# Laying a state-space scan out by channels and states, in a kernel that runs it beside attention

## The chip, the cores and the metric

The kernel runs on one core of one Trainium2 chip. The core has five engines with a queue each, worked off in order: TensorE (PE) for matmuls, VectorE (DVE), ScalarE (ACT) and GpSimd (POOL) for elementwise work, SyncE (SP), which here issues nearly every DMA. The metric is the time of one execution in device microseconds. Of the kernel before, three runs took 6126.20, 6140.09 and 6140.57 us; the median is 6140.09.

## The reference

Two layers over x of 4 images, 128 channels, 64 x 64 pixels. Layer 0 normalises, convolves 3 x 3 by channel, and then treats the 128 channels as four chunks of 32 channels; each chunk of each image is one sequence of 4096 tokens for the same state-space block, with 64 inner channels d and 16 states n. Layer 1 is softmax attention (4 heads over 4096 tokens) and a mixture of 8 experts, 2 per token. What the change touches is this:

```python
delta = jax.nn.softplus(dt @ dt_proj_w.T + dt_proj_b)
A = -jnp.exp(A_log)
dA = jnp.exp(delta[..., None] * A)
dBu = delta[..., None] * Bm[:, :, None, :] * xin[..., None]
def step(h, inp):
    dA_t, dBu_t, C_t = inp
    h = dA_t * h + dBu_t
    y = jnp.einsum('bdn,bn->bd', h, C_t)
    return (h, y)
...
y = jnp.transpose(ys, (1, 0, 2)) + D_skip * xin
out = y * jax.nn.silu(z) @ out_proj_w.T
```

So delta and xin depend on the channel, B and C on the state, A on both; y is a sum over the states.

## The kernel before, in words

**Blocks and halves.** An image is cut into 8 blocks of 512 tokens. Two of the four chunks are worked on at a time: they are a half p of a block, and their 2 x 64 = 128 (chunk, channel) pairs lie on the 128 partitions. 4 images x 8 blocks x 2 halves x 16 give 1,024 scan units.

**A unit** is one state n of all 128 pairs. `fetched` (L724) loads B and C of that state for both chunks, repeated over the 64 channels, from `bcd` in DRAM into `rows` (512 KB). `decayed` (L734) makes da = exp(delta * A) on ACT. `scan` (L739) is three DVE operations of 128 x 512: h = B * du, where du = delta * xin; the scan along the tokens, starting from `states`; hc = C * h. `scanned` (L752) adds the skip term once the sum over the states, y, is complete.

**The sum over states** is made in PSUM: PE multiplies hc by the identity and accumulates 16 products per half. In image 0 each hc goes to PE. In the images after, POOL first adds each pair of hc, and PE gets 8 sums per half.

**The slot loop** (L1113) writes the order of the work out by hand: every engine's instructions are chained in the order in which they are recorded. There is one unit per slot. Beside the units run two lanes of tasks written as generators. A `yield` ends a half-slot: `advance(lane, True)` and `advance(lane, False)` each run one stage. Lane Y makes the inputs of later blocks: `first_norm` (y0), `conv` (xn), and `inputs` (L675) twice per block, where ACT makes softplus in the four steps e, e, ln, delta, and POOL finishes delta and du in five operations. Lane X finishes blocks after their scans: `closed` (L761) makes queries, keys and values, and `divided` and `finished` (L946) close the attention and do the experts. A stage that yields "short" (the experts' products and their evictions acc) lets lane X take a second pair of stages in a slot. Attention of an image starts when its last block is closed: per slot, four score products (sc), two exponentials of 128 x 1024 (pT) on ACT, and four products with the values (av, 64 columns each, two column tiles) a slot later. An fp32 product of PE is two records in the profile.

A slot before records, in this order: the sends collected so far and `rows` of the unit three slots ahead (SP); lane X's second half (its evictions); sc and pT; lane Y; the y products that are due, and `scanned`; the copy of the last state of the previous unit (ACT); da of the next unit (ACT); the three scan operations (DVE) and the pair's add (POOL); lane Y; av; lane X's first half (its products).

`until` (L1074) runs before a unit's rows are fetched: while the inputs of its half are not done, it runs the half-slots of both lanes, out of the slot's order.

## Time and profile before

| what | value |
|---|---|
| median of three runs | 6140.09 us |
| profiled execution: its own time, its span | 6135.26 us, 6133.5 us |
| granted TensorE clock, mean | 0.921 |
| busy: PE, DVE, ACT, POOL | 5188.5, 4197.3, 3952.4, 1925.1 us |
| DVE scan operations (h and the two forms of scan, hc) | 795.9, 1299.8 + 176.9, 801.2 us |
| POOL's adds of hc pairs | 384, 557.1 us |
| DMA moved | 928.55 MB, of it 1,024 x 512 KB rows |

The page has the busy time of each engine, a row of 40 slices of the span with the busy share in tenths, the chain of work that ended last followed back to its start, and the costliest groups of instructions with what ended the idle time before them. All lane and loop operations are recorded by one helper, so they share the line L445; they are told apart by the names of what they write and read. A window gives busy time by engine for a stretch of the span.

### The profile page before, as it was taken

The numbers are of one execution on the slowest core, as the hardware profiler recorded it, in microseconds if no ns is written. First come the engines' busy times: TensorE is split into PE (matmuls) and PEld (weight loads), VectorE is DVE, ScalarE is ACT, GpSimd is POOL, SyncE is SP. The second block draws the span as 40 slices with busy tenths as digits, with TensorE's granted clock in tenths as the row PEclk, the third lists the DMA queues.
The fourth block names the chain that finished last, engine by engine and source line by source line (L and its number), as shares of the span: only waits on it lengthen the run. The fifth ranks groups of instructions, "written<-read, shape, count | busy, mean of one in ns | idle before, by whom it ended". The sixth has DMA issues, their size and how long they took to land.

```text
span 6133.5 us, 60705 instructions
## 1 busy us (share of the span) xinstructions
PE 5188.5 (85%) x18378; PEld 2135.6 (35%) x18378; DVE 4197.3 (68%) x7155; ACT 3952.4 (64%) x6052; POOL 1925.1 (31%) x1757
## 2 busy tenths in 40 slices
PE   4666665698899989889999898999888898999996
PEld 2222222233333333333333333333333333333332
DVE  4888887788888877778888777888777772021112
ACT  3445544577777767677777676777777765655652
POOL 2334323444344334333444344344333320000000
PEclk7777777799999999999999999999999999999996
DMA  3444554555455535555555554555554542212210
GB/s 99 163 174 164 187 178 152 171 190 170 168 184 178 188 134 181 167 170 179 187 178 181 178 168 168 177 167 174 174 167 165 170 158 79 79 64 72 74 66 13
DMA packets 359137, 928.55 MB, mean 151 GB/s; under 512 B 37633, under 2 KB 120978, under 8 KB 358802
## 3 DMA queue, kind: packets, MB, share of 16 engines
q1 hardware_dynamic: 357634, 923.80, 44.7%
q8 instruction: 148, 2.42, 0.2%
q14 instruction: 187, 1.53, 0.1%
q10 hardware_dynamic: 1168, 0.80, 0.0%
HBM read 806.95 MB, written 100.66 MB: 148 GB/s over the span
## 4 chain that ended last, share of the span: by engine, by line
PE 43%; DVE 33%; ACT 12%; POOL 5%; issue 5%; DMA 2%; SPq 0%; DVEq 0%; ACTq 0%; POOLq 0%
PE av L445 18%; DVE h L445 15%; PE ps_X L445 10%; PE sc L445 9%; DVE hc L445 5%; DVE acc L445 5%; PE y L445 4%; ACT pT L445 3%; PE ps_Y L445 3%; DVE cm L445 3%; ACT L445 2%; ACT xt L445 2%; POOL rsX L445 2%; POOL rsY L445 1%; ACT da L445 1%
## 5 line engine op out<-in xcount | busy, mean ns | idle before, releaser
L445 ACT ACTIVATE pT<-sc 128x1024 f32<-128x1024 f32 x2048 | 1986.7, 1024 | 881.2 <-PE sc L445 876.3
L445 PE MATMUL av<-pT,v 128*64 128x512 f32 x8192 | 2027.1, 616 | 0.0
L445 DVE TENSOR_TENSOR_SCAN h<-da,state,h 128x512 f32<-128x512 f32 x896 | 1299.8, 1451 | 244.0 <-ACT da L445 157.8
L445 PE MATMUL sc<-qs,ks 128*128 128x512 f32 x4096 | 1335.2, 444 | 124.5 <-ACT pT L445 77.4
L445 POOL TENSOR_TENSOR hc<-hc 128x512 f32<-128x512 f32 x384 | 557.1, 1451 | 1707.3 <-DVE hc L445 1542.9
L445 PEld LDWEIGHTS sc<-qs,ks 128*128 128x128 f32 x4096 | 714.3, 192 | 726.5 <-ACT pT L445 367.8
L445 PE MATMUL y<-hc,ident 128*128 128x512 f32 x1280 | 804.2, 718 | 181.7 <-DVE hc L445 172.5
L445 PEld LDWEIGHTS av<-pT,v 128*64 128x64 f32 x8192 | 506.9, 139 | 1168.0 <-issue 1140.3
L445 DVE TENSOR_TENSOR hc<-rows,h 128x512 f32<-128x512 f32 x1024 | 801.2, 782 | 70.9 <-DVE h L445 1.4
L445 DVE TENSOR_TENSOR h<-rows,du 128x512 f32<-128x512 f32 x1024 | 795.9, 777 | 32.3 <-POOL du L445 29.2
L445 ACT ACTIVATE da<-delta,amat 128x512 f32<-128x512 f32 x1024 | 750.2, 734 | 25.8 <-DVE h L445 24.3
L445 DVE SCALAR_TENSOR_TENSOR acc<-ps_X,pr,acc 128x128 f32<-128x128 f32 x1024 | 358.4, 350 | 304.6 <-PE ps_X L445 276.8
L445 ACT ACT_TABLE_LOAD x318 | 408.0, 1283 | 101.8 <-PE sc L445 92.1
L445 POOL TENSOR_SCALAR rsX<-mvX 128x4 f32<-128x4 f32 x97 | 52.4, 540 | 1224.3 <-DVE mvX L445 1222.7
L445 PE MATMUL ps_X<-w_ew,xf 128*128 128x512 f32 x512 | 304.3, 678 | 126.0 <-DVE acc L445 123.9
L445 PEld LDWEIGHTS y<-hc,ident 128*128 128x128 f32 x1280 | 260.3, 222 | 419.8 <-DVE hc L445 302.8
L445 DVE RECIPROCAL rden<-ps_X 128x8 f32<-128x8 f32 x64 | 13.1, 205 | 566.9 <-PE ps_X L445 566.9
L445 ACT COPY state<-h 128x1 f32<-128x1 f32 x896 | 176.3, 197 | 269.6 <-DVE h L445 269.2
L445 ACT ACTIVATE xt<-ps_Y,shiftY,rsY 128x128 f32<-128x128 f32 x380 | 142.9, 460 | 174.3 <-POOL shiftY L445 158.2
L445 DVE TENSOR_TENSOR_SCAN h<-da,h 128x512 f32<-128x512 f32 x128 | 176.9, 1382 | 57.0 <-ACT da L445 45.8
L445 POOL TENSOR_SCALAR rsY<-mvY 128x4 f32<-128x4 f32 x95 | 43.5, 458 | 532.7 <-DVE mvY L445 528.0
L445 PE MATMUL ps_Y<-ident,xt 128*128 128x128 f32 x380 | 74.7, 329 | 159.8 <-ACT xt L445 159.5
(197 smaller groups left out, 4766.6 us busy)
## 6 DMA issues: line engine op xcount, KB each, us to landing
rows<-bcd SPq DMA_DIRECT2D x1024, 512.0 KB, 4.2
ks<-kd SPq DMA_DIRECT2D x256, 512.0 KB, 5.6
v<-vd SPq DMA_DIRECT2D x256, 256.0 KB, 5.9
qs<-qd SPq DMA_DIRECT2D x64, 512.0 KB, 5.8
pairs<-xn SPq DMA_DIRECT2D x128, 128.5 KB, 2.4
qd<-hi SPq DMA_DIRECT2D x32, 512.0 KB, 6.8
qd<-lo SPq DMA_DIRECT2D x32, 512.0 KB, 5.9
vd<-vst SPq DMA_DIRECT2D x32, 512.0 KB, 7.4
```

Source lines behind the costliest of these rows:

```text
L445: return lambda *args, **kw: queued(op(*args, **kw))
```

## The change

Rows are laid out anew. A unit is now 8 channels with all 16 states of one chunk; eight units cover a chunk's 64 channels, sixteen a half. B and C depend on the state and the chunk alone, so one tile `bcs` (512 KB) holds both for eight units, while `rows` now brings delta and du of the unit's 8 channels, repeated over the 16 states. For that, `inputs` writes delta and du into one tile `dd` and sends it to DRAM as `ddd`, each row twice (1 MB), two slots after POOL's operations (four yields more). da is computed from the fetched delta, so it reads `rows` too. The sum over states crosses partitions: PE multiplies hc by the 0/1 matrix `sel`, 32 columns wide; the four units of a group write to four strips of 32 partitions of y, and four groups accumulate. POOL's pair adds are gone in all images. The channels are reordered on the partitions to match (`place`).

In the slot, the state copy and da of the next unit now come before sc and pT, and the scan comes before lane X's evictions, unless the stage is a short one. e and ln move to the scratch buffers of lane Y, `lost` shares du's place; da has two buffers and hc six.

```diff
@@ -92,7 +92,7 @@
-    amat = const.tile([P, NST], F32, name="amat")
+    amat = const.tile([P, P // NST], F32, name="amat")
...
@@ -697,60 +697,81 @@
         bcd = dram.tile([2, NST, 2 * BLK], F32, name="bcd", bufs=4)
         send(bcd.rearrange("c n (k q) -> (c n k) q", k=2), bc)
-        e = mix.tile([P, BLK], F32, name="e")
+        dd = mix.tile([P, 2, BLK], F32, name="dd")
+        delta, du = dd[:, 0, :], dd[:, 1, :]
+        e = tmp("Y", "e")
         scalar.activation(e, ps, AF.Abs, bias=dtb)
         scalar.activation(e, e, AF.Exp, scale=-1.0)
-        ln = mix.tile([P, BLK], F32, name="ln")
+        ln = tmp("Y", "ln")
         scalar.activation(ln, e, AF.Ln, bias=1.0)
-        delta = mix.tile([P, BLK], F32, name="delta", bufs=2)
         scalar.activation(delta, ps, AF.Relu, bias=dtb)
         yield
         yield
-        lost = mix.tile([P, BLK], F32, name="lost")
+        lost = du
         gpsimd.tensor_scalar(lost, e, 1.0, -1.0, ALU.add, ALU.add)
         gpsimd.tensor_sub(lost, e, lost)
         gpsimd.tensor_add(ln, ln, lost)
         gpsimd.tensor_add(delta, delta, ln)
-        du = mix.tile([P, BLK], F32, name="du", bufs=2)
         gpsimd.tensor_mul(du, delta, xin)
-        in_of[b, i, p] = xin, zs, delta, du, bcd
+        yield
+        yield
+        yield
+        yield
+        ddd = dram.tile([P, 2, 2 * BLK], F32, name="ddd", bufs=4)
+        send(ddd, dd.rearrange("p k q -> p (k q)")[:, None, :].to_broadcast([P, 2, 2 * BLK]))
+        in_of[b, i, p] = xin, zs, ddd, bcd
         yield
         yield
         yield
     states = [mix.tile([P, 2, NST], F32, name=f"state{k}") for k in range(2)]
-    def fetched(b, i, p, n):
-        bcd = in_of[b, i, p][4]
+    def fetched(b, i, p, k):
+        ddd, bcd = in_of[b, i, p][2:]
+        if k % 8 == 0:
+            w = mix.tile([P, 2, BLK], F32, name="bcs", bufs=2)
+            sync.dma_start(
+                out=w.rearrange("p k q -> p (k q)"),
+                in_=bcd[k // 8][None].to_broadcast([P // NST, NST, 2 * BLK]),
+            )
+            chunk[0] = w
         w = mix.tile([P, 2, BLK], F32, name="rows", bufs=4)
+        at = 32 * (k % 4) + 8 * (k // 4)
         sync.dma_start(
             out=w.rearrange("p k q -> p (k q)"),
-            in_=bcd[:, n, :][None].to_broadcast([DI, 2, 2 * BLK]),
+            in_=ddd[at : at + 8].rearrange("d c q -> (d c) q")[:, None, :].to_broadcast(
+                [NST, P // NST, 2 * BLK]
+            ),
         )
-        return w
-    def decayed(b, i, p, n):
-        da = mix.tile([P, BLK], F32, name="da", bufs=3)
-        scalar.activation(da, in_of[b, i, p][2], AF.Exp, scale=amat[:, n : n + 1])
+        return w, chunk[0]
+    chunk = [None]
+    def decayed(k, w):
+        da = mix.tile([P, BLK], F32, name="da", bufs=2)
+        scalar.activation(da, w[:, 0, :], AF.Exp, scale=amat[:, k % 8 : k % 8 + 1])
         return da
-    def scan(b, i, p, n, w, da):
-        du = in_of[b, i, p][3]
+    def scan(b, i, p, k, w, bc, da):
         h = mix.tile([P, BLK], F32, name="h", bufs=3)
-        vector.tensor_mul(h, w[:, 0, :], du)
+        vector.tensor_mul(h, bc[:, 0, :], w[:, 1, :])
         vector.tensor_tensor_scan(
-            out=h, data0=da, data1=h, initial=0.0 if i == 0 else states[b % 2][:, p, n : n + 1],
+            out=h, data0=da, data1=h, initial=0.0 if i == 0 else states[b % 2][:, p, k : k + 1],
             op0=ALU.mult, op1=ALU.add,
         )
-        hc = mix.tile([P, BLK], F32, name="hc", bufs=5)
-        vector.tensor_mul(hc, w[:, 1, :], h)
+        hc = mix.tile([P, BLK], F32, name="hc", bufs=6)
+        vector.tensor_mul(hc, bc[:, 1, :], h)
         return h, hc
     def scanned(b, i, p, y):
-        xin, zs, delta, du, bcd = in_of.pop((b, i, p))
+        xin, zs = in_of.pop((b, i, p))[:2]
         vector.scalar_tensor_tensor(xin, xin, dsk, y, ALU.mult, ALU.add)
         gpsimd.tensor_mul(zs, xin, zs)
         gated[b, i, p] = zs
@@ -1109,14 +1130,20 @@
     units = [(b, i, p, n) for b, i in blocks for p in range(2) for n in range(NST)]
     rows, decays, old, due = {}, {}, None, deque()
-    even, y_of, waiting, groups, image, slot = None, {}, None, None, 0, 0
+    terms, y_of, waiting, groups, image, slot = [], {}, None, None, 0, 0
     while slot < len(units) or due or waiting or groups or image < B or lanes["X"] or running:
         flush()
         for ahead in range(slot if slot == 0 else slot + 3, min(slot + 4, len(units))):
             until(("in", *units[ahead][:3]))
             rows[ahead] = fetched(*units[ahead])
-        advance("X", True)
+        if old:
+            (b, i, p, n), h = old
+            if i < NB - 1:
+                scalar.copy(states[b % 2][:, p, n : n + 1], h[:, BLK - 1 : BLK])
+            old = None
+        for ahead in range(slot if slot == 0 else slot + 1, min(slot + 2, len(units))):
+            decays[ahead] = decayed(units[ahead][3], rows[ahead][0])
         if groups is None and image < B and ("closed", image, NB - 1) in done:
             groups = attention(image)
             image += 1
@@ -1124,40 +1151,35 @@
         if groups is not None and group is None:
             groups = None
+        taken = short["X"] and advance("X", True)
+        if slot < len(units):
+            unit = units[slot]
+            h, hc = scan(*unit, *rows.pop(slot), decays.pop(slot))
+            old = unit, h
+            terms.append(hc)
+            if len(terms) == 4:
+                due.append((slot + 1, unit, terms))
+                terms = []
+        if not taken:
+            advance("X", True)
         task = running.get("Y") or (lanes["Y"][0] if lanes["Y"] else None)
         more = short["X"] and (task is None or task[0][0] != "in") and advance("X", False)
         advance("Y", False)
         while due and due[0][0] <= slot:
-            _, unit, term, first = due.popleft()
-            b, i, p, n = unit
-            if first:
+            _, (b, i, p, k), four = due.popleft()
+            q = k // 4
+            if q == 0:
                 y_of[b, i, p] = ps_y.tile([P, BLK], F32, name="y")
-            mm(y_of[b, i, p], ident, term, first, n == NST - 1)
-            if n == NST - 1:
+            for g, term in enumerate(four):
+                mm(y_of[b, i, p][32 * g : 32 * g + 32, :], sel[:, q, :], term, q == 0, q == 3)
+            if q == 3:
                 scanned(b, i, p, y_of.pop((b, i, p)))
                 done.add(("scan", b, i, p))
                 if p == 1:
                     lanes["X"].appendleft((("closed", b, i), closed(b, i), []))
-        if old:
-            (b, i, p, n), h = old
-            if i < NB - 1:
-                scalar.copy(states[b % 2][:, p, n : n + 1], h[:, BLK - 1 : BLK])
-            old = None
-        for ahead in range(slot if slot == 0 else slot + 1, min(slot + 2, len(units))):
-            decays[ahead] = decayed(*units[ahead])
-        if slot < len(units):
-            unit = units[slot]
-            h, hc = scan(*unit, rows.pop(slot), decays.pop(slot))
-            old = unit, h
-            b, i, p, n = unit
-            if b == 0:
-                due.append((slot + 1, unit, hc, n == 0))
-            elif n % 2 == 0:
-                even = hc
-            else:
-                gpsimd.tensor_add(even, even, hc)
-                due.append((slot + 2, unit, even, n == 1))
         advance("Y", True)
         if more:
             advance("X", True)
...
@@ -1205,16 +1227,24 @@
         return a.reshape(1, -1)
+    j, d = np.divmod(np.arange(DI), 8)
+    place = [32 * (j % 4) + 8 * (2 * c + j // 4) + d for c in range(2)]
     def twice(a):
-        return np.repeat(a, 2, axis=0)
+        w = np.empty((P,) + a.shape[1:], a.dtype)
+        w[place[0]] = w[place[1]] = a
+        return w
     z = np.zeros((P, P), np.float32)
     inx, inz = z.copy(), z.copy()
     wout = np.zeros((P, 2, P), np.float32)
     wbc = np.zeros((P, 2, NST, 2), np.float32)
+    sel = np.zeros((8, NST, 4, 4, 8), np.float32)
+    for q in range(4):
+        sel[:, :, q, q] = np.eye(8)[:, None, :]
     xdt, dtT = np.zeros((4, P), np.float32), np.zeros((4, P), np.float32)
     for c in range(2):
-        d = slice(c, P, 2)
+        d = place[c]
         for p in range(2):
             s = slice(64 * p + 32 * c, 64 * p + 32 * c + 32)
             inx[s, d] = c0["in_proj_w"][:DI].T
...
-        "wbc": wbc.reshape(P, -1), "alog": twice(c0["A_log"]),
+        "wbc": wbc.reshape(P, -1), "sel": sel.reshape(P, 4, 32),
+        "alog": c0["A_log"].reshape(8, 8, NST).transpose(1, 2, 0).reshape(P, 8),

```

## The prediction

> **What bounds the kernel now.** I read the page's totals and slices first, then busy time by stage, the chain of waits, the groups, VectorE's (DVE's) waits and one slot's timeline.
>
> ```profile
> PE 5188.5 (85%) x18378; PEld 2135.6 (35%) x18378; DVE 4197.3 (68%) x7155; ACT 3952.4 (64%) x6052; POOL 1925.1 (31%) x1757
> PE   4666665698899989889999898999888898999996
> DVE  4888887788888877778888777888777772021112
> ...
> 100.00:1000.00 900.00, 579.20 (x1187) 225.58 (x1186) 754.13 (x1077) 442.00 (x862) 316.04 (x281) 0.76 0.49 167
> 1100.00:5000.00 3900.00, 3475.79 (x12914) 1449.88 (x12914) 3112.18 (x5072) 2841.38 (x4395) 1531.60 (x1345) 0.96 0.52 174
> 5030.00:6133.00 1103.00, 1006.10 (x3950) 409.21 (x3948) 201.64 (x726) 582.29 (x668) 24.22 (x51) 0.94 0.19 63
> ```
>
> The last three lines are stages (busy PE, weight loads, DVE, ACT, POOL, then clock, DMA share, GB/s). Image 0 has the scan alone: DVE leads with 754 of 900 us. From 1100 to 5000 the scans of images 1 to 3 run beside the attention of the image before: PE leads with 3476 of 3900 (89%), DVE has 80%, ACT 73%. The end is attention alone and PE's (91%). The 1,024 scan units give slots of 3.8 us in image 0 and 5.1 us in the middle.
>
> ```profile
> PE 43%; DVE 33%; ACT 12%; POOL 5%; issue 5%; DMA 2%; SPq 0%; DVEq 0%; ACTq 0%; POOLq 0%
> PE av L445 18%; DVE h L445 15%; PE ps_X L445 10%; PE sc L445 9%; DVE hc L445 5%; DVE acc L445 5%; PE y L445 4%; ACT pT L445 3%; PE ps_Y L445 3%; DVE cm L445 3%; ACT L445 2%; ACT xt L445 2%; POOL rsX L445 2%; POOL rsY L445 1%; ACT da L445 1%
> ...
> L445 PE MATMUL y<-hc,ident 128*128 128x512 f32 x1280 | 804.2, 718 | 181.7 <-DVE hc L445 172.5
> L445 POOL TENSOR_TENSOR hc<-hc 128x512 f32<-128x512 f32 x384 | 557.1, 1451 | 1707.3 <-DVE hc L445 1542.9
> ```
>
> The chain passes from PE to DVE and back; y has 4% of it, the scan's h and hc 20%. A y product is two records, so 1280 records are 640 products: 256 in image 0, and 384 later, where POOL first adds the hc in pairs.
>
> ```profile
> DVE acc L445 <- PE ps_X L445: 177.7, 65, 8.7
> DVE h L445 <- ACT da L445: 146.0, 89, 6.5
> DVE pr L445 <- PE ps_X L445: 92.0, 19, 13.0
> DVE xin L445 <- PE y L445: 63.7, 28, 10.0
> DVE rden L445 <- PE ps_X L445: 47.3, 27, 5.9
> DVE stX L445 <- PE ps_X L445: 28.8, 12, 2.9
> ...
> 3003.02 1.02 PE L445 MATMUL y<-hc,ident 128*128 128x512 f32 x2
> 3003.97 0.20 PEld L445 LDWEIGHTS av<-pT,v 128*64 128x64 f32 x4 [0.76 <-issue]
> ...
> 3003.97 1.94 PE L445 MATMUL av<-pT,v 128*64 128x512 f32 x8
> ```
>
> DVE's waits in the middle (total us, times, longest) are evictions of lane X and late decays, each with a scan queued behind it. In the timeline one y product takes 1.02 us; four 64-column products (av, eight records) take 1.94. So two column tiles already run at once.
>
> **Part by part.**
>
> *The sum over states.* Each y product becomes 32 columns wide; four of them, to four column strips, make a group: 64 groups in image 0 and 192 later, where 256 and 384 products stood. If four tiles overlap as two do, a group costs about one product. The chain's 4% is 245 us; split as y's PE time lies (342 us in image 0, 421 later) it is 110 and 135. Saved: 3/4 of 110 and 1/2 of 135, **150 us**. Ends: with no overlap nothing in image 0 and 384 more products later, +135 by the chain (+421 if all of PE's time counts); with PE's whole later time counted, 82 + 210 = 292 saved. I take the chain's value, with full overlap, since av is the nearest row.
>
> The Trainium skill (TensorE: Matmul & The Clock Gate, Measured speedup vs the span model) gives three column tiles at 512 columns 2.38x, not 3x; at that efficiency a group would cost about 1.28 us, and I estimate 24 us of the 150 to be lost. Its page TensorEngine Tiling (Array Packing), Key Properties, speaks against the change: a change of tiling mode drains the array. The trace shows av beginning 0.95 us after the y before it began, about as long as the product, so I would charge no more by it.
>
> *POOL's 384 adds go* (557 us, 29% of POOL). The three scan operations average 777, 1451 and 782 ns against medians of 684, 1284 and 692 where nothing disturbs them; that excess is 0.35 us by 1,024, 358 us. The adds' share of POOL makes it 104; all the middle's excess in the three scan operations (about half of 358) would be 180. h and hc have 41% of their busy time on the chain (with decimals 15.2% and 5.4% of 6133, so 1264 of 3074), so 43 to 74: **60 us**, ends 0 and 180. zs and the lane's rs chains also stand behind fewer POOL operations; nothing is added for that.
>
> *Lane X behind the scan.* DVE's scan no longer queues behind an eviction that waits for PE, except the experts' (acc, marked short), which stay ahead. The waits for pr, xin, rden, stX and smaller ones are 275 us in the middle, da's 146; image 0 has 50 for da, 26 for xin and some 25 more. Of these 520 us only what lies on the chain counts. By DVE's 33% it is 170; as some of it turns into PE waiting for a later eviction I take **100**, ends 0 and 275.
>
> *What that delays.* PE's next X product now waits for an eviction behind a scan (0.68 + 1.28 + 0.69 = 2.65 us on DVE) or two exponentials (2 x 1.0 us on ACT). In the middle PE has sc (1.2), av (1.94), y and lane Y ahead of it, so only the four xt (4 x 0.46 = 1.84 us) come late, 72 times by about 0.5: 40. At the end, without y or Y, PE reaches that product after some 2.8 us and ACT after 3.2 to 4.4: 4 us for each of nine blocks, 35. **+75**, ends 0 and +150. State copy and da stand before the exponentials now, so pT waits for the scan of the slot before. ACT waited 23 us for that in the middle, in a later place; nothing for it.
>
> *Lane Y is four half-slots longer per input.* A block's tasks count 13 + 11 + 27 + 13 = 64 half-slots, in 32 slots that offer 64, and the unit 32 is asked for at slot 29. Walking the lanes through the program, the loop that forces lane Y forward runs 150 times in place of 60 (38 and 36 at the start), three per block and ten at the last block of images 0 to 2 instead of six or seven. Most rounds hold only empty steps and the send; in 15 blocks they pull one or two X stages forward, some 2.7 us each (four expert evictions of 0.35 and the product after them), 40. That ends lane X seven slots sooner: the end has 310 slots in 1103 us, so **-25**.
>
> *Delta through DRAM.* SP sends 1 MB per half block and rows waits for it; before, rows read bcd, and delta stayed on chip. In the trace du is ready 17 to 24 us before the scan that needs it. The nearest writes: out 256 KB in 2.1 us, qd 512 KB in 6.8; for 1 MB I take 5 to 9. rows lands in 4.2, da is 0.73, h's product 0.68: 11 to 15 us. The send goes out with SP's place three slots ahead and rows' buffer frees about five scans ahead, 14 us at image 0's shortest slots (2.8) and over 20 in the middle. So it is hidden but for the first block (+11: scan 0 came 2.5 us after du) and the last block of each image (in image 0 du ended 6.4 us before the scan, so about 7 lost; less later): 30 with what is forced there. Queued behind it on SP are the next rows, ks and v; ks and v are asked for three slots (15 us) ahead and land in under 6. bcs (512 KB per eight units) and the sends add 128 MB to 929, at a DMA share of 0.52: 0, end +100. da now needs rows a slot sooner, two slots after issue, 7.6 us at least against 4.2. Together with the forced rounds **+70**, ends +20 and +250.
>
> Table loads, other PE work and the attention stay. Sum: -150 - 60 - 100 + 75 + 70 - 25 = **-190**, from the profiled execution's own 6135 to 5945. The median of the runs shown is 5 us above that execution: **5950**.
>
> **Rivals.**
> *Tiles do not overlap* (8%): y gives +135 instead of -150: 6235, up to 6500. Against it: av's 1.94 us for four.
> *Two by two* (12%): a group costs two products; image 0 saves 55, the middle nothing: 6045.
> *The round trip through DRAM shows* (14%), the slower side. All of SP's queue stops while rows waits for the send; then ACT stops at da, ahead of pT, so PE stops. For it: the trace's forced place in image 1 left DVE 8.1 and 13.0 us idle. It decides where a block loses over 190/32, 6 us, beyond what I count: a write above about 14 us, or rows far over 4.2. At 10 us per block: 6270; range 6150 to 6350.
> *Evictions late* (9%): PE waits at the upper end for lane X (+150) and DVE's wait merely moves (0 saved): 6125, 6060 to 6180.
> *Both ends relieved* (12%): PE's 292 and 150 from DVE's waits: 5760.
> My forecast's case has 45%, with a range of 5830 to 6030 of its own.
>
> **Numbers.** 5740 to 6230 leaves out about a fifth: the best of the both-relieved case, the worse halves of the two slow ones. 0.3% (18 us) is about what this measurement can tell from no change. Faster: 45 + 12 + 12 and half of the late-eviction case, with a little of mine taken off, 0.72; same 0.04; slower 0.24.
>
> **What would show it.** Four y records starting together and y's PE time in the middle near 210 us; else a rival. POOL near 1370 us, h and hc means nearer 690, 1290 and 700. DVE's waits for pr, xin, rden and da mostly gone, and PE or ACT waits for lane X grown by under 100 us. No wait of da or h for rows above a few us per block, and the first scan about 11 us later. I am wrong if pT or da waits long for rows, or if PE's products to ps_X wait for evictions by hundreds of us.

## The result, and the profile after

The changed kernel takes 6408.2 us (median of 4 runs, 6400.2 to 6413.5) against 6139.3 for the kernel before: ratio 1.0442, interval 1.0424 to 1.0460. It is 269 us slower, where 190 us less had been forecast. The profiled execution has a span of 6411.6 us.

The page's totals, slices and DMA queue of the changed kernel (busy time and instructions; tenths of forty slices; packets, MB and share of sixteen DMA engines), and its stages (busy PE, weight loads, DVE, ACT, POOL, then clock, DMA share, GB/s):

```profile
PE 5017.3 (78%) x19146; PEld 1968.5 (31%) x19146; DVE 4049.5 (63%) x7155; ACT 3970.7 (62%) x6052; POOL 1351.7 (21%) x1373
...
PE   3554444488888878788888888888888889999996
...
DVE  3877786777777767777778667777777673121122
...
DMA  4777776778686867677786858677777782222220
...
q1 hardware_dynamic: 392594, 1058.09, 63.4%
```

```profile
100.00:1000.00 900.00, 432.49 (x1042) 141.36 (x1042) 688.92 (x964) 393.37 (x773) 262.85 (x245) 0.62 0.76 188
1100.00:5000.00 3900.00, 3223.66 (x12828) 1278.51 (x12828) 2853.32 (x4906) 2710.32 (x4191) 951.28 (x948) 0.93 0.74 191
```

No engine has more to do than before by over 20 us, POOL has 573 us less (its adds of 557 are gone), yet all of them are less busy per microsecond. What went up is the DMA share: 0.49 to 0.76 in image 0, 0.52 to 0.74 in the middle. Before, the queue moved 923.80 MB in 44.7% of 6133 us; now 1058.09 MB take 63.4% of 6412. That is 15% more bytes and 48% more packet time.

The chain of waits and the groups, after:

```profile
PE 36%; DVE 22%; ACT 15%; DMA 14%; POOL 6%; issue 5%; SPq 1%; DVEq 0%; ACTq 0%; POOLq 0%
...
L445 ACT ACTIVATE da<-rows,amat 128x512 f32<-128x512 f32 x1024 | 748.4, 732 | 523.4 <-DMA rows<-ddd 488.8
...
L445 DVE TENSOR_TENSOR h<-bcs,rows 128x512 f32<-128x512 f32 x1024 | 810.2, 791 | 203.2 <-DMA rows<-ddd 203.2
...
L445 PE MATMUL y<-hc,w_sel 128*32 128x512 f32 x2048 | 423.0, 756 | 117.6 <-DVE hc L445 117.6
```

DMA has 14% of the chain where it had 2%, and the wait for rows stands in front of da and h, as the sign named in the prediction for being wrong. ACT and DVE sat idle 692 us in all until rows landed. The sum over states did what it was meant to: y's PE time went from 804 to 423 us.

The wait has a place. These are SP's, ACT's and DVE's timelines around the start of one half block in image 0 (start, duration, instruction, idle time before it and its releaser):

```profile
691.81 0.55 SPq L445 DMA_DIRECT2D rows<-ddd  x1
692.41 1.08 SPq L445 DMA_DIRECT2D bcs<-bcd  x1
693.60 13.44 SPq L445 DMA_DIRECT2D rows<-ddd  x5
```

```profile
698.68 0.72 ACT L445 ACTIVATE da<-rows,amat 128x512 f32<-128x512 f32 x1 [2.39 <-DMA rows<-ddd]
699.31 0.17 ACT L445 COPY state<-h 128x1 f32<-128x1 f32 x1
705.75 0.72 ACT L445 ACTIVATE da<-rows,amat 128x512 f32<-128x512 f32 x1 [6.27 <-DMA rows<-ddd]
```

```profile
705.76 0.69 DVE L445 TENSOR_TENSOR h<-bcs,rows 128x512 f32<-128x512 f32 x1 [3.40 <-DMA rows<-ddd]
```

bcs was issued at 692.4, the rows of the half's first unit right behind it at 693.6. In the DMA records bcs landed 11.1 us after issue and those rows 12.1 us after issue, and ACT and DVE stood still before them until then. A transfer's landing is counted there in steps: bcs has one step just after its issue and eight from 9.5 to 11.1 us, and those rows have sixteen, eight from 6.4 to 7.6 us and eight from 10.5 to 12.1. Over the whole run, 324 of the 489 us that ACT waited for rows in front of da fall on the first of a half's sixteen units, 53 times. The other 64 bcs go out ahead of a half's ninth unit, and there ACT waits 18 us in all: by the same records the first units' rows land in 10.4 us in image 0 and are wanted 5.7 us after their issue, the ninth units' land in 8.5 and are wanted after 10.5 (medians).

### The profile page after: what moved, and what is told of

Same layout as the page of the kernel before. It is cut to its first block, busy times and chain, and to the rows that moved or that the text cites. A ratio compares the mean times of both kernels' runs of the same rounds, so it can differ in the third digit from the quotient of the medians.

```text
span 6411.6 us, 62726 instructions
## 1 busy us (share of the span) xinstructions
PE 5017.3 (78%) x19146; PEld 1968.5 (31%) x19146; DVE 4049.5 (63%) x7155; ACT 3970.7 (62%) x6052; POOL 1351.7 (21%) x1373
## 3 DMA queue, kind: packets, MB, share of 16 engines
q1 hardware_dynamic: 392594, 1058.09, 63.4%
## 4 chain that ended last, share of the span: by engine, by line
PE 36%; DVE 22%; ACT 15%; DMA 14%; POOL 6%; issue 5%; SPq 1%; DVEq 0%; ACTq 0%; POOLq 0%
PE av L445 13%; PE ps_X L445 9%; DVE h L445 9%; DMA rows<-ddd 8%; PE sc L445 8%; ACT pT L445 5%; DVE acc L445 4%; PE ps_Y L445 4%; DVE hc L445 3%; ACT L445 3%; PE y L445 2%; ACT xt L445 2%; POOL rsX L445 2%; DMA gn<-in_x 1%; POOL dd L445 1%
## 5 line engine op out<-in xcount | busy, mean ns | idle before, releaser
L445 DVE TENSOR_TENSOR_SCAN h<-da,state,h 128x512 f32<-128x512 f32 x896 | 1206.4, 1346 | 312.8 <-ACT da L445 228.6
L445 ACT ACTIVATE da<-rows,amat 128x512 f32<-128x512 f32 x1024 | 748.4, 732 | 523.4 <-DMA rows<-ddd 488.8
L445 DVE TENSOR_TENSOR h<-bcs,rows 128x512 f32<-128x512 f32 x1024 | 810.2, 791 | 203.2 <-DMA rows<-ddd 203.2
L445 DVE TENSOR_TENSOR hc<-bcs,h 128x512 f32<-128x512 f32 x1024 | 794.5, 776 | 51.6 <-DVE h L445 0.5
L445 PE MATMUL y<-hc,w_sel 128*32 128x512 f32 x2048 | 423.0, 756 | 117.6 <-DVE hc L445 117.6
L445 POOL TENSOR_TENSOR zs<-xin,zs 128x512 f32<-128x512 f32 x64 | 107.0, 1671 | 1224.0 <-DVE xin L445 1204.2
L445 POOL TENSOR_SCALAR dd<-e 128x512 f32<-128x512 f32 x64 | 125.9, 1967 | 858.3 <-ACT e L445 802.3
L445 PE MATMUL ps_X<-ident,xt 128*128 128x128 f32 x388 | 109.2, 345 | 215.0 <-ACT xt L445 205.6
```

What stands on the lines that cost most here:

```text
L445: return lambda *args, **kw: queued(op(*args, **kw))
```

## The experiments

Numbers of several kernels side by side, worked out from the DMA and instruction records; pairs are image 0 / the middle. "rows" and "bcs" are median us from issue to landing, "packet" the mean ns of a 4 KB packet, "first unit" ACT's wait for the rows of a half's first unit, us in all; for the last kernel "bcs" is the later of its two transfers, from the first one's issue.

```
                              time    rows      bcs        packet     first unit
before                        6139   4.0/4.3    -          189/194       -
order, quarter of y           5943   4.0/4.6    -          187/194       -
changed                       6408   6.6/6.8  10.5/10.8    269/259     119/205
rows from two DRAM rows       6264   4.9/5.0   9.5/ 9.6    208/202      90/130
bcs two slots earlier         6372   7.7/8.2   9.6/ 8.8    270/261      70/ 87
no bcs after the first half   6177   5.9/5.9    -          252/241      54/ 43
two rows, no bcs              6127   4.1/4.3    -          189/187      42/ 29
bcs from 128 rows             6231   6.7/7.1   7.7/ 8.8    248/239      70/ 84
state-major                   6158   5.8/6.0   6.8/ 7.1    260/247      53/ 55
state-major, bcs in 8 + 8     6324   6.5/6.5  10.1/10.0    280/258     111/165
```

**The order alone.** The kernel before with the changed kernel's slot order: state copy, decay and scan moved ahead of the attention step, lane X behind the scan unless short.

```
-        advance("X", True)
+        (state copy, decayed)          # as in the changed kernel
         ...
+        taken = short["X"] and advance("X", True)
+        (scan; due as before)
+        if not taken:
+            advance("X", True)
```

> The kernel before with the new slot order alone (state copy and decays ahead of the exponentials, scan ahead of lane X's evictions unless short); layout, DMAs and y products as before. Theory A (the loss is in the transfers of the new layout, the order is worth a little): 6060 to 6140 us, DVE's waits for pr, rden, stX and da clearly below the 275 + 146 us of before, PE's waits for lane X up by less than 100. Theory B (the order itself costs, since PE waits for evictions behind the scan and behind the exponentials): above 6250.

Measured: 6066.1 us, ratio 0.9901 (0.9882 to 0.9921), 62 us faster than the 6127.9 that the kernel before took beside it. DVE's waits from 1100 to 5000 us, to be read against those shown of before:

```profile
DVE acc L445 <- PE ps_X L445: 160.1, 68, 8.3
DVE h L445 <- ACT da L445: 132.3, 51, 7.9
DVE lo L445 <- ACT hi L445: 73.1, 30, 3.9
DVE pr L445 <- PE ps_X L445: 48.6, 17, 13.0
DVE xin L445 <- PE y L445: 29.6, 21, 8.7
...
DVE rden L445 <- PE ps_X L445: 22.7, 9, 15.5
```

pr went from 92 to 49, xin from 64 to 30 and rden from 47 to 23; da's hardly fell (146 to 132). The end got 14 us longer, as forecast in kind (35).

**The new layout with the old order.** The changed kernel, with lane X back ahead of the scan.

```
-        (state copy, decayed)
+        advance("X", True)
         ...
-        taken = short["X"] and advance("X", True)
-        (scan)
-        if not taken: advance("X", True)
         (y products)
+        (state copy, decayed, scan)
```

> The changed kernel with the slot order of before (lane X's evictions first, decays and scan late); everything else as changed. Theory A: still well above before, 6300 to 6480, since bcs, ddd and the rows' reads stay; the waits of da and h for rows shrink somewhat, as da is asked for later in a slot, but DVE's old waits return. Theory B: 6150 or less.

Measured: 6409.8 us, ratio 1.0465 (1.0446 to 1.0483), as the changed kernel. Here the order is worth nothing, as two things cancel. The wait of da and h for rows with the old order, and DVE's wait for da from 1100 to 5000 us with the old order and in the changed kernel:

```profile
  DMA rows<-ddd: 422.5, 147
```

```profile
DVE h L445 <- ACT da L445: 284.2, 147, 15.0
```

```profile
DVE h L445 <- ACT da L445: 165.0, 62, 10.4
```

With the old order da is asked for later, and the wait for rows is 423 us in place of 692; but DVE's old waits are back, in the same stretch 284 for da where the changed kernel has 165, and 102 in front of rden where it has 73. What the new order saves at the evictions it pays to rows.

**The forecast without the DRAM route.** The order alone, and of every four hc only the last goes to PE as a full product, with no additions on POOL.

```
-            if b == 0:
-                due.append((slot + 1, unit, hc, n == 0))
-            elif n % 2 == 0:
-                even = hc
-            else:
-                gpsimd.tensor_add(even, even, hc)
-                due.append((slot + 2, unit, even, n == 1))
+            if n % 4 == 3:
+                due.append((slot + 1, unit, hc, n == 3))
```

> The kernel before with the new slot order, and of the sum over states only every fourth hc goes to PE, none through POOL: 4 products of 1.02 us per half and no pair adds, as much PE and POOL work as the changed kernel has, in the old layout with the old transfers (three quarters of the states are left out of y). It measures what y and POOL's adds were worth by themselves, against 6066 us for the order alone. If my terms of 150 and 60 us hold, 5830 to 5900. If that work is mostly not on the path: 5980 to 6060.

Measured: 5942.8 us, ratio 0.9689 (0.9673 to 0.9705). This has the changed kernel's order, no adds either, about its work for y (PE 324 us, 423 there), and delta on chip; three quarters of the states are left out of y. Less y and no adds are worth 123 us on top of the order. By stage, image 0 gains nothing (977.8 us with the order alone, 990.5 here), images 1 to 3 gain 69, 21 and 55. Its image 0 and middle, and the same two stages of the order alone:

```profile
100.00:1000.00 900.00, 392.86 (x809) 157.03 (x808) 748.17 (x1045) 432.94 (x842) 293.47 (x270) 0.64 0.48 165
1100.00:5000.00 3900.00, 3466.16 (x13255) 1456.13 (x13256) 2989.12 (x5275) 2975.17 (x4546) 1019.17 (x995) 0.96 0.53 179
```

```profile
100.00:1000.00 900.00, 579.72 (x1176) 223.12 (x1174) 760.82 (x1073) 438.00 (x857) 300.96 (x280) 0.75 0.49 166
1100.00:5000.00 3900.00, 3503.07 (x13209) 1483.83 (x13209) 3123.53 (x5160) 2905.49 (x4453) 1575.87 (x1355) 0.97 0.53 176
```

In image 0 PE loses a third of its busy time, and DVE, which leads there, stays as it was; the clock that PE is granted falls from 0.75 to 0.64. So what the changed kernel has besides, the DRAM route with its empty steps above all, costs 6408 - 5943 = 465 us, not 269.

**No wait for delta.** The same pattern of reads from a DRAM tile filled once; delta is still sent.

```
+    fixed = dram.tile([P, 2, 2 * BLK], F32, name="fixed", bufs=1)
+    sync.dma_start(out=fixed, in_=taps...to_broadcast([P, 2, 2 * BLK]))
-            in_=ddd[at : at + 8]...
+            in_=fixed[at : at + 8]...
```

> The changed kernel, but rows reads a DRAM tile written once at the start, in the same 16-row pattern; ddd is still sent but nobody waits for it. The scan so works on fixed numbers, not on delta and du. Theory A1: little changes outside the first halves of blocks: 6280 to 6400. Theory A2 with the round trip as the cause: the first rows of a block come 5 us earlier, 28 to 32 blocks, waits of the first unit of first halves gone (62 us in image 0 and 46 after on ACT, of 324 at first units), second halves unchanged: 6150 to 6280. If first units of second halves still wait, bcs ahead of them is the cause there.

Measured: 6407.0 us, ratio 1.0454 (1.0436 to 1.0471). ACT's first-unit waits are 127 and 199 us, unchanged. The trip of delta through DRAM is hidden as forecast; the rival of the round trip had the right sign and saw ACT stop at da for rows, but the send is not what rows is late for.

**Rows from two DRAM rows.** Each rows tile reads two rows of delta 64 times in place of sixteen stored rows eight times.

```
-            in_=ddd[at : at + 8].rearrange("d c q -> (d c) q")[:, None, :].to_broadcast(
-                [NST, P // NST, 2 * BLK]
-            ),
+            in_=ddd[at][None].to_broadcast([DI, 2, 2 * BLK]),
```

> The changed kernel, but each rows transfer reads two rows of ddd (one channel's delta and du, both copies) 64 times each, the pattern that rows had before, instead of 16 rows 8 times each; so all 8 channels of a unit get one channel's delta and du, and the other channels are left out of the scan. Same bytes, same wait for ddd. Theory A1 (the 16-row read pattern is what slows each 4 KB packet from a mean of 189 ns to 259-269 and keeps the 16 DMA engines full behind bcs): 4 KB packets back near 190 ns, rows landing in 4 to 5 us instead of 6.6, 6000 to 6150 us. Theory A2 (the packets are slow because of bcs or the longer queue, or the loss is the round trip through DRAM): packets and landing hardly change, above 6330.

Measured: 6264.1 us, ratio 1.0217 (1.0200 to 1.0234), 144 us back with the same bytes. A 4 KB packet fell from 269 to 208 ns (medians 159 before, 271 in the changed kernel), and rows land in 5.0 us. The time lies between the two that were expected (up to 6150, above 6330): the packets are a part of the loss and not the whole.

**bcs taken away,** alone and with two-row reads: bcs is fetched for the first half only and kept.

```
-        if k % 8 == 0:
+        if k % 8 == 0 and k // 8 not in kept:
...
-            chunk[0] = w
+            kept[k // 8] = w
+        chunk[0] = kept[k // 8]
```

> The changed kernel with bcs fetched only for the first half of all; later units scan with that B and C, so the B and C of all later halves are left out of the transfers and of the result. Rows as changed, 16 rows. Theory C: first units hardly wait, 6230 to 6310. Theory D: 64 MB fewer of 1063, rings less full, 6300 to 6370. If bcs is innocent: above 6380.

> Both at once: rows from two DRAM rows 64 times each, and bcs fetched only for the first half (other channels' delta and du, and later B and C, are left out). If the transfers are the whole loss and the rest of the change gains as forecast (y, POOL's adds, the order, which alone gave 61 us): 5900 to 6060. If something else costs too (lane Y's longer inputs and forced rounds, the send, da's earlier need of rows): 6100 to 6200.

Measured: 6177.4 us, ratio 1.0077 (1.0059 to 1.0095), and 6126.9, ratio 0.9997 (0.9986 to 1.0008). 126 transfers, 66 MB of 1058, cost 231 us, and 137 where rows reads two rows; two-row reads bring 50 more, not another 144, so the two share most of their price.

**bcs two slots earlier.** The resident tile is issued five slots ahead of its half and not three.

```
+        if slot + LEAD < len(units) and units[slot + LEAD][3] % 8 == 0 and slot > 0:
+            resident(*units[slot + LEAD])        # LEAD = 5
```

> The changed kernel with each bcs transfer issued two slots earlier than the first rows that follow it (as soon as its half's B and C are in DRAM); same bytes. Theory C (the first units of a half wait because their rows stand behind bcs in the DMA rings): the waits of da and h for rows at first units (324 and 179 us) fall below 120 and 70, rows 0 to 2 of a half land in 5 to 8 us instead of 10 to 13, 6270 to 6340. Theory D (the rings are short of time as a whole, packets being slow, and whatever stands ahead matters little): above 6380, waits only move to other units.

Measured: 6372.2 us, ratio 1.0388 (1.0361 to 1.0414). ACT's first-unit waits halve (324 to 157 us), but the waits for rows at units 14 and 15 of a half, those now behind bcs, grow from 50 to 263. The hole moves with bcs: it is not that bcs itself is late, but that other transfers stand behind it.

**Distances in DRAM.** 512 bytes between delta's rows; 16 KB from row to row; 16 KB for B and C too.

```
-        ddd = dram.tile([P, 2, 2 * BLK], F32, name="ddd", bufs=4)
+        ddd = dram.tile([P, 2, 2 * BLK + 128], F32, name="ddd", bufs=4)[:, :, 0 : 2 * BLK]
                               (+ 3072 for the 16 KB step)
```

> The changed kernel with 512 B between the 4 KB rows of ddd, so that the 16 rows of a rows transfer no longer lie at multiples of 4 KB. Theory E (the packets are slow because 16 neighbouring rows at 4 KB steps meet in the same part of the memory): 4 KB packets fall from a mean of 258-269 ns to near 205, about the time of the two-row run, 6264 us, 6240 to 6300. Theory F (it is the number of different rows read at once): no change, 6380 to 6430.

> The changed kernel with the 4 KB rows of ddd at 16 KB steps instead of 4 KB (the step at which the keys' 64 rows lie, whose packets run at a median of 159 ns). Theory G (the 16 rows of one transfer lie in 64 KB and meet in the same part of the memory; the 512 B of the run before were too little to spread them): 4 KB packets from 258-269 ns down to about 205, time like the two-row run, 6230 to 6300. Theory F (it is how often a row is read again by one engine, or how many rows are read, wherever they lie): packets unchanged, 6370 to 6430.

> The same 16 KB step for ddd and also for bcd's rows, from which bcs reads (the columns of wbc are reordered so that B and C of a state are stored by two sends). Theory G: bcs lands in 6 to 7 us instead of 10.5 and packets near 190 ns: 6120 to 6230. Theory F: as the 16 KB run of rows alone, above 6350.

Measured: 6404.8, 6395.4 and 6384.8 us, ratios 1.0439, 1.0424 and 1.0414 (the last 1.0396 to 1.0433). The packets still take 262 and 252 ns with the 16 KB step. Neighbouring addresses are not the cause, or under a tenth of it.

**Rows straight from SBUF,** with no DRAM tile, no send and no empty steps; the outermost size of the transfer's access pattern is 8 (8 outer entries).

```
-            in_=ddd[at : at + 8]... [NST, P // NST, 2 * BLK]
+            in_=dd[at : at + 8].rearrange("p k q -> p (k q)")[:, None, :].to_broadcast(
+                [P // NST, NST, 2 * BLK]
+            ),
```

> The changed kernel without ddd: rows is fetched by DMA straight from dd in SBUF (8 rows repeated 16 times), dd has two buffers and h two instead of three, and the four additional yields are gone. It takes away the 1 MB send, its round trip and lane Y's longer inputs, and reads SBUF instead of DRAM. If reading 16 DRAM rows is what makes packets slow, packets from SBUF are near 160-190 ns and bcs alone stays: 6150 to 6280. If eight source rows spread over half the DMA engines only, rows take longer still: above 6400.

Measured: 10468 us, ratio 1.7074 (1.7025 to 1.7122). rows lands in 24 us. Its DMA slices, queue, and the wait for rows (all views of this kernel's page and of the tile rows):

```profile
DMA  3444445455555555555555555555555555542221
...
q1 hardware_dynamic: 366994, 990.94, 48.0%
```

```profile
  DMA rows<-dd: 8137.0, 1467
```

DVE and ACT wait 8.1 ms for rows, and yet the sixteen DMA engines are never much above half busy. This turned the question: at any moment seven and a half to eight packets are under way, where other transfers have sixteen. Its rows begin with eight outer entries, and so does bcs in the changed kernel (eight copies of sixteen rows); the changed kernel's rows, with delta stored twice, begin with sixteen. How much of the 24 us is the eight entries, and how much the source in SBUF, was not separated. The start of the changed kernel and of the state-major kernel below, from the DMA records (packets under way on the mean, and mean ns of the 4 KB packets under way, in the half microsecond from each time):

```
changed kernel: ddd issued 102.7, bcs 103.3, rows 107.9, 108.5, 109.1, 109.7
   from 104.5   105.5  106.5  107.0  107.5  108.0  108.5  109.5  110.5  112.0
   way   15.8    16.1   12.4    8.0    8.2    8.2    8.2   16.3   16.3   16.8
   ns     160     194    277    223    185    253    249    305    562    573
state-major: ddd issued 99.2, bcs 99.6, rows 102.2, 102.8, 103.5, 104.1
   from 100.5   101.0  101.5  102.0  102.5  103.0  103.5  104.0  104.5  105.0
   way   16.1    15.8   16.1   16.4   16.4   12.1    1.7   10.4   15.1   16.4
   ns     172     242    213    229    262    273    308    162    202    256
```

In the changed kernel bcs, once it is alone, keeps 8 packets under way for two microseconds, and when rows join, the packets under way take up to 573 ns on the mean.

The Trainium skill (DMA: Bandwidth & Descriptors, Rules for kernel authors) says this outright: a leading zero-stride broadcast of c < 16 copies confines the whole transfer to at most c engines. The 8.0 to 8.2 packets agree with it, and so do the landings: all 128 bcs of the changed kernel come in eight steps after the one at issue, all 1,024 rows in sixteen. What it is worth here the next three runs measure.

**State-major.** The partitions of a scan row are 16 states of 8 channels in place of 8 channels of 16 states. bcs then begins with sixteen states, delta is stored once, and rows reads its eight rows in turn, sixteen times.

```
-        ddd = dram.tile([P, 2, 2 * BLK], F32, name="ddd", bufs=4)
-        send(ddd, dd.rearrange("p k q -> p (k q)")[:, None, :].to_broadcast([P, 2, 2 * BLK]))
+        ddd = dram.tile([P, 2 * BLK], F32, name="ddd", bufs=4)
+        send(ddd, dd.rearrange("p k q -> p (k q)"))
-                in_=bcd[k // 8][None].to_broadcast([P // NST, NST, 2 * BLK]),
+                in_=bcd[k // 8][:, None, :].to_broadcast([NST, P // NST, 2 * BLK]),
-            in_=ddd[at : at + 8].rearrange("d c q -> (d c) q")[:, None, :]...
+            in_=ddd[at : at + 8][None].to_broadcast([NST, P // NST, 2 * BLK]),
```

> The changed kernel with the rows of a unit ordered by state first and channel second: each rows transfer reads 8 different DRAM rows in turn, 16 times over (ddd is stored once, 512 KB), and bcs reads 16 rows 8 times each, with 16 outer entries instead of 8, so that it runs on 16 DMA engines and not on 8. Same result. If an engine that reads the same row over and over is what slows packets, rows land in about 4 to 5 us as with two rows, and only bcs has slow packets: 6170 to 6270. If it is the number of different rows, rows stay at 6 to 7 us; bcs on 16 engines alone then gives 6280 to 6350. Above 6380 neither matters.

Measured: 6158.2 us, ratio 1.0038 (1.0023 to 1.0052): 250 of the 269 us are back. But a 4 KB packet still takes 260 and 247 ns. So most of the 250 us do not come from cheaper packets, and the time lies below all that was expected; bcs now lands in sixteen steps, in 7 us in place of 10.7, and the first-unit waits are 53 and 55 us, as without bcs. As two things differ, the next two runs change bcs alone, in both layouts.

**bcs from 128 rows.** The changed kernel, with B and C stored in eight copies.

```
-        bcd = dram.tile([2, NST, 2 * BLK], F32, name="bcd", bufs=4)
-        send(bcd.rearrange("c n (k q) -> (c n k) q", k=2), bc)
+        bcd = dram.tile([2, P // NST, NST, 2 * BLK], F32, name="bcd", bufs=4)
+        for c in range(2):
+            send(bcd[c].rearrange("r n (k q) -> (n k) r q", k=2),
+                 bc[32 * c : 32 * c + 32, :][:, None, :].to_broadcast([32, P // NST, BLK]))
-                in_=bcd[k // 8][None].to_broadcast([P // NST, NST, 2 * BLK]),
+                in_=bcd[k // 8].rearrange("r n q -> (r n) q"),
```

> The changed kernel with B and C written to DRAM in eight copies, so that the resident tile is read as 128 rows one after another and not as 8 outer entries of 16 rows; 56 MB more is written, delta and its rows are as in the changed kernel. Theory A (a transfer with 8 outer entries is spread over half of the DMA engines, lands late and holds the rows behind it): bcs lands in about 7 us in place of 10.7, ACT's waits for the rows of a half's first unit fall from 324 to about 110 us as without bcs, and the time is 6160 to 6260. Theory B (what the state-major layout gained was delta stored once and its rows read in turn): no better than 6370.

**State-major with bcs in 8 + 8.**

```
+            for n in range(0, NST, 8):
                 sync.dma_start(
-                out=w..., in_=bcd[k // 8][:, None, :].to_broadcast([NST, P // NST, 2 * BLK]),
+                    out=w...[8 * n : 8 * n + 64, :],
+                    in_=bcd[k // 8][n : n + 8][:, None, :].to_broadcast([8, 8, 2 * BLK]),
```

> The state-major kernel (6158 us) with the resident tile of B and C fetched in two transfers of 8 outer entries each in place of one of 16; bytes, rows and order are the same. Theory A: each of the two keeps to half of the engines, the later of the two lands in about 10 us in place of 7, ACT's first-unit waits go from 109 to some 250 us, and the time is 6300 to 6400. Theory B: 6140 to 6190, as before the split.

Measured: 6230.9 us, ratio 1.0151 (1.0134 to 1.0168), and 6324.0, ratio 1.0309 (1.0292 to 1.0326). The queue and the group of da on the page of the first, then of the second, then of the state-major kernel:

```profile
q1 hardware_dynamic: 423314, 1116.82, 65.3%
...
L445 ACT ACTIVATE da<-rows,amat 128x512 f32<-128x512 f32 x1024 | 747.9, 731 | 370.1 <-DMA rows<-ddd 335.2
```

```profile
q1 hardware_dynamic: 385426, 1024.54, 62.0%
...
L445 ACT ACTIVATE da<-rows,amat 128x512 f32<-128x512 f32 x1024 | 748.3, 732 | 458.0 <-DMA rows<-ddd 421.5
```

```profile
q1 hardware_dynamic: 385426, 1024.54, 61.1%
...
L445 ACT ACTIVATE da<-rows,amat 128x512 f32<-128x512 f32 x1024 | 748.3, 732 | 269.6 <-DMA rows<-ddd 229.4
```

The waits of da and h for rows are 440, 587 and 291 us (692 in the changed kernel). With bcs read as 128 rows the changed kernel gets 177 us back although it moves 59 MB more, at a higher queue share (65.3% for 63.4%). With bcs in transfers of eight entries the state-major kernel loses 166, with the same bytes and nearly the same queue share; the later of the two lands in 10 us, and both come in eight steps, the 128 rows in sixteen. Both directions agree. The theory that stood against it (delta stored once and read in turn) falls as the whole account, but keeps a part: with bcs on eight entries in both, the state-major kernel is 84 us faster than the changed one, with bcs on sixteen or more 73. Of that part neither the fewer bytes (34 and 92 MB), nor the order of the reads, nor the shorter send (3.0 us for 5.3) was tried alone. The mean packet moves along with bcs too (269 to 248, 260 to 280 ns in image 0); that was not separated from the entries. What decides is not how busy the DMA engines are on the average (the slower kernel of the first pair has the lower share), but that half of them hold a long transfer while rows, spread over all sixteen, wait for the slower half: the steps at 693.6 above show it.

**The four empty steps of the input task.** They were added so that delta is sent before the scan asks. Taken out of the kernel with two rows and no bcs, and of the state-major kernel; then with bcs two slots earlier.

```
         gpsimd.tensor_mul(du, delta, xin)
-        yield
-        yield
-        yield
-        yield
```

> The run with two-row reads and no bcs (6127 us), and in addition without the four yields of inputs, so that lane Y fits its slots again and the forced rounds fall back to about those of before; SP may then stand at the send until POOL has finished. The same parts of the computation are left out as there. If the forced rounds and the longer lane are what eats the gain of y and POOL: 6040 to 6085. If they cost nothing, 6110 to 6140, and the gain of y and POOL's adds is simply not on the path.

> The same, and without the four yields of inputs, worth 55 us where the transfers were cheap: 40 to 70 us below the run with state-major rows, 6110 to 6220 if that one comes as hoped. If SP's stand at the send then costs as much as lane Y gains, the two are equal within 20 us.

> The run with state-major rows and the shorter lane Y, and bcs issued two slots ahead of the first rows (36 us with the 8-engine bcs). If the first units of a half still wait behind bcs, 10 to 40 us below that run; if bcs on 16 engines no longer holds them, equal within 15 us. Below 6066 it would beat the order alone.

Measured: 6072.4 us, ratio 0.9898 (0.9878 to 0.9917), 55 faster than with the steps; 6175.2, ratio 1.0072 (1.0056 to 1.0089), 17 slower; 6136.7, ratio 1.0006 (0.9995 to 1.0018), 38 faster than that. Without the steps images 1 to 3 are 49, 50 and 19 us shorter in the first of these, image 0 is 35 longer (ACT now waits for rows at units 7 and 13), and the end is 41 us longer (1089.1 to 1129.7). In the state-major kernel ACT's wait in front of da for rows doubles (229 to 475 us), which takes the gain. So the steps do hide the round trip, for a price that is seen (55 us) where rows are on time.

## Why the prediction was wrong, step by step

**The step that failed** is the one on the resident rows and the sends: "128 MB to 929, at a DMA share of 0.52: 0, end +100", and with it "rows lands in 4.2". It priced a transfer by its bytes and the mean share of sixteen engines. The first half of those bytes, bcs, costs 231 us when it is taken away; 166 to 177 are the eight outer entries, which keep it on half the engines for 10.7 us with the rows of the half's first unit right behind it. The check of the lead, "two slots after issue, 7.6 us at least against 4.2", failed on both sides: in the lines above those rows landed 12.1 us after issue, and ACT was free for them after 5.9 (two of the shortest slots that the prediction names itself, 2.8 us, make 5.6). The end of +100 was too low as no transfer of the loop before is of that kind: each of them lands in sixteen steps. The diff did show it: `to_broadcast([P // NST, NST, ...])` begins with 8, and rows, with delta stored twice, with 16.

The other part is rows' own packets: the 4 KB packets took 189 to 194 ns on the mean where a tile reads two rows 64 times, as before, and 269 and 259 where it reads sixteen rows eight times. Two-row reads gave back 144 us with bcs and 50 without it. Without both the time is 6127, 281 us less.

**The sum over states and POOL's adds**: four tiles do overlap when they start together. Eight y records then take about one product, 1.07 us (the prediction names 1.28 as an estimate beside its sum), with no gap to the products of other widths beside them; the second group is one in image 0 at a granted clock of 0.5, the third, of which the first of four products is shown, one where PE comes before the hc do:

```profile
3019.43 1.13 PE L445 MATMUL ps_Y<-g,w_fc2T 128*128 128x512 f32 x2 [0.84 <-ACT g L445]
3020.48 1.07 PE L445 MATMUL y<-hc,w_sel 128*32 128x512 f32 x8
3021.48 1.94 PE L445 MATMUL av<-pT,v 128*64 128x512 f32 x8
...
868.63 1.94 PE L445 MATMUL y<-hc,w_sel 128*32 128x512 f32 x8
...
889.65 1.91 PE L445 MATMUL y<-hc,w_sel 128*32 128x512 f32 x2 [6.14 <-DVE hc L445]
```

The rivals without full overlap fall for 220 of the 256 groups, those that start their four products together. Over the run y's PE time is 423 us, more than the 296 that the same split gives (342/4 + 421/2): 170 for 85 in image 0, 253 for 210 later. Of the 170 us, 103 are 22 groups whose products start apart, 4.7 us each on the mean; most of the rest goes with the clock (1.07 us a group at 1.0, 1.94 at 0.5). The gain was mis-sized: 150 + 60 forecast, 123 measured. Images 1 to 3 gave 145 against the forecast 128 (half of 135, and 60), but image 0 nothing where 82 was counted, as DVE leads it. Without the adds the means of h, scan and hc were to near 690, 1290 and 700 ns; the changed kernel has 791, 1346 and 776, so only the scan followed (1451 before).

**The order**: -25 forecast (-100 and +75), -62 measured, in the layout of before. The waits that it was to shorten did shorten; of what it delays only the end was measured by itself, 14 us for 35. In the changed kernel it is worth nothing, as it also asks for rows earlier.

**Lane Y and the round trip**: the end got 20 us shorter (1109.6 to 1089.4; -25 forecast), the first scan came 13 us later (11 forecast), the 1 MB write lands in 5.2 to 5.4 us (5 to 9 assumed), and the trip itself is hidden. The empty steps cost more than the 40 counted for forced rounds less 25 at the end: 55 in the one pair where rows were on time.

Without the DRAM route these terms give 5943, 7 us from the forecast 5950, partly by chance, as the forecast's +70 for that route is not in it. The 465 us between it and the changed kernel are 281 for bcs and the many-row reads, 55 for the empty steps, and 129 that stay **open**: they lie between the kernel with two rows, no bcs and no empty steps (6072) and the one with delta on chip (5943). ACT's idle time in front of da, 310 us (267 of them for rows) against 29, is likely to be in it; that was not separated. Open, too, is why a packet costs more when many rows are read (neither their distance nor their order explains it).

The version to use is the kernel before with the new order alone: 6066 us, 1.0% less than before.

## What to carry to other kernels

Before pricing an added transfer by its bytes, look at the outermost size of its access pattern: with eight entries it used half of the engines here, took 10.7 us in place of 7, and held what was issued right behind it. Its price is then the work that waits behind it at that place: 66 MB of 1058 cost 231 us with the mean DMA share at three quarters, and most of the waiting behind it lay at the first units, where rows had 6 to 8 us of lead, and next to none at the ninth, where they had 10 and more. If such a hole moves when the transfer is issued earlier and does not close, mend the access pattern, or give what stands behind it more lead.

## What the runs showed of the hardware

4 KB packets were dearer where the rows tiles read many different rows of DRAM. Their mean in image 0 is 189 ns with two rows (before) and 208 (the changed kernel with two), 269 with sixteen rows each read eight times on end, 260 with eight read in turn; without bcs it is 189 with two rows and 252 with sixteen; 512 bytes more (269) or 16 KB (262) from row to row change it little. At the end of the kernels, with attention alone, 4 KB packets take 188 to 198.

In image 0 PE's granted clock was lower in the kernels that gave it less to do: 0.76 with 579 of 900 us busy, 0.64 with 393, 0.62 with 432 in the changed kernel. A cut in PE's work there did not shorten the stage (977.8 to 990.5 us).
